# Two graph-attention layers on one core: gathers moved ahead of a norm's root in the first graph, means written in place, and one graph's row of Q made by TensorE

## The chip, the cores and the metric

The kernel runs on one core of a Trainium2 chip. The metric is the device time of one execution in microseconds; lower is better. A time below is the median of several runs, and beside it stands one further execution that was profiled.

## The reference, cut to what matters

The input is x of 16 graphs of 1024 nodes with 256 features, and one adjacency matrix of 1024 x 1024. There are two layers, each with a layer norm in front and a residual behind. The core of it:

```python
h = jnp.maximum(_layernorm(x), 0.0)
# layer 0
out = relu(h @ mlp1_w + mlp1_b);  residual = out            # 256 -> 512
out = elu(_gat(relu(out), None, W_fc, a_fc)) + residual     # dense attention: every node with every node
out = relu(out @ mlp2_w + mlp2_b); residual = out           # 512 -> 256
out = elu(_gat(relu(out), adj, W_hand, a_hand)) + residual  # masked attention
x = x + relu(out)
# layer 1
h = jnp.maximum(_layernorm(x), 0.0)
x = x + relu(masked attention of h with adj, W, a)
```

A `_gat` computes `h = inp @ W`, two numbers per node `f1 = h @ a[:F]` and `f2 = h @ a[F:]`, the scores `leaky_relu(f1[i] + f2[j])`, a softmax over j, and `elu(att @ h)`. All arithmetic is float32.

## The kernel before, in words

Nodes lie on partitions: a graph is 8 tiles of 128 nodes (`NT`), or two halves of 4 tiles (`TH`). Every graph goes through norm, mlp1, dense attention (class `Dense`), mlp2, masked attention a (`Gnn0`), a second norm and masked attention b (`Gnn1`). Neighbouring graphs overlap.

**Dense attention without the 1024 x 1024 matrix.** Because leaky_relu has two slopes, a node's sum over all others is one part over the nodes with a large f2 and one over those with a small f2. The kernel sorts the rows of h by f2: `rank` counts on DVE, `scatter` writes the rows to DRAM in order (an indirect DMA from POOL), `read_sorted` reads them back as `xs`. `sum_before` and `sum_behind` make running sums on DVE, `write_table` and `carry` write them to two tables in DRAM, `fine` and `coarse`. How many nodes lie on one side of node i comes from `sign` (a Sign activation with an accumulator on ACT, one for each tile of nodes) and `count`. Then `gather` (line 642) fetches for each tile of nodes a row of `fine` for each node, and adds a row of `coarse` to it, both by indirect DMAs that POOL issues. `share` (lines 654 to 657, DVE) makes the factors, `mean` (line 664 on ACT, line 666 on DVE) the weighted mean `hp` of 513 columns, `merge` (lines 713 to 717: TensorE transposes, a minimum on DVE, two exponentials on ACT) and `merge_end` (line 723 on DVE, line 724 on POOL) apply elu and add it to `resT`. `mlp2` (line 731) needs all four chunks c of a half of `resT`.

Graph 0 is special. Its first half (4 tiles) is computed in the direct way, `product` (line 695) and `product_mean` (lines 702 to 706), because TensorE has nothing else to do while the tables are made; its second half goes by the tables. `split` is true for graph 0 alone. Its sums lie in `got`, two buffers of two tiles each, which have the tag "hm" (two buffers in all); the means lie in tiles with the tag "hp" (four buffers), which both halves use.

**Rows of Q.** Masked attention needs exp of a per-node value as a row on all partitions. For graphs 1 to 14 (`AHEAD`), `send` transposes it to a line, copies it on ACT and stores it to DRAM (lines 243 to 246), and `row(True)` reads it back on SP's queue to all 128 partitions (line 360). For graphs 0 and 15, `row` makes it by eight TensorE transposes of a broadcast column (line 238) and two copies on ACT (line 365). `weight` (line 375, DVE) makes the attention weights from the row, `product` (line 385) multiplies them.

**What sets the order.** Everything is written out by hand in a table of steps with due times:

```python
def at(lo, hi, steps):
    for i, step in enumerate(steps):
        table.append((lo + (hi - lo) * i / len(steps), len(table), step))
```

The steps run in the order of these times when the program is made, and TensorE, DVE, ACT and SP take their instructions in exactly that order. POOL's instructions, the issue of indirect DMAs among them, keep the table's order too, except that scatters may pass each other. A due time is only a place in that order: an instruction starts when its operands are there and what is ahead of it on its engine is done.

The lines of graph 0's ramp that the change touches, before:

```python
def first_norm(t0, b):                       # called as first_norm(0, 2) for the third graph
    n = norm1[b]
    lo = t0 - (62 if b == 2 else 33.5)
    at(lo, lo + 1, n.stats_steps(0))         # four bn_stats/bn_aggr on DVE, then the root on POOL
...
gathers(d, 1, START + 108, START + 114)      # START is -168; d is graph 0
at(START + 135, START + 135, [partial(d.share, 1)])
at(START + 135.5, START + 137, each(d.mean, [1], range(TH)))
merges(START + 138.2, d, 1)
at(START + 144, START + 158, each(e.sign, range(NT)))    # e is graph 1
```

Here `stats_steps(0)` stands at START + 106, so the root (lines 267 and 268) comes ahead of graph 0's gathers on POOL.

Of the kernel before, what the change touches and what calls it, by code (L numbers as in the profile page):

```python
# [8 lines left out]
F32 = mybir.dt.float32  # L9
# [8 lines left out]
P = 128  # L18
# [13 lines left out]
def fast_path(ctx: ExitStack, tc: tile.TileContext, alarm, x, adj, w1, b1, w2, b2, w_fc, a_fc,  # L32
# [24 lines left out]
    NT = N // P  # L57
# [3 lines left out]
    TH = HALF // P  # L61
    R = H + 2
    K = H + 1
# [3 lines left out]
    work = ctx.enter_context(tc.tile_pool(name="work", bufs=2))  # L67
# [154 lines left out]
# [3 lines that stand above are left out]
# [212 lines left out]
    class Dense:  # L437
# [221 lines left out]
        def mean(self, h, u):  # L659
            n = TH // len(self.got[h])  # L660
            got, den = self.got[h][u // n][:, u % n, :], self.dens[h]
            name = f"{self.b}_{h}_{u}"
            part = work.tile([P, K], F32, tag="part", name=f"part_{name}")
            nc.scalar.activation(part, got[:, :K], AF.Copy, scale=den[:, 1, u:u + 1])
            hp = self.hps[h, u] = work.tile([P, K], F32, tag="hp", name=f"hp_{name}", bufs=TH)
            nc.vector.scalar_tensor_tensor(hp, got[:, K:], den[:, 0, u:u + 1], part,
                                           op0=OP.mult, op1=OP.add)

# [104 lines left out]
    def each(f, *ranges):  # L773
        out = [()]
        for r in ranges:
            out = [o + (i,) for o in out for i in r]
        return [partial(f, *o) for o in out]

    def first_norm(t0, b):

        n = norm1[b]
        lo = t0 - (62 if b == 2 else 33.5)
        at(lo, lo + 1, n.stats_steps(0))
        at(t0 - 13, t0 - 9, n.stats_steps(1))
        n.turn_at(t0 - (14.5 if b == 2 else 22), 0, 4 if b == 2 else 7)
        n.turn_at(t0 + 0.2, 1, 4)
# [49 lines left out]
    def gathers(d, h, lo, hi):  # L836
        at(lo, lo + 4, each(d.gather, [h], [0], range(TH)))
        at(hi, hi + 7, each(d.gather, [h], [1], range(TH)))
# [20 lines left out]
    def merges(lo, d, h):  # L859
        at(lo, lo + 9.2, each(d.merge, [h], range(HC)))  # L860
        at(lo + 2.5, lo + 11.7, each(d.merge_end, [h], range(HC)))

    def second_mlp(t0, b, after=0):
        d, m = dense[b], gnn0[b]
        for i, lo in enumerate((102.5, 104.8, 113, 116.5)):
            lo += t0 - 3.4 * last(b)
            at(lo, lo, [partial(d.mlp2, i // FC, i % FC)])
        t0 += after
        at(t0 + 135, t0 + 142, each(m.project, range(NT)))
        at(t0 + 141.9, t0 + 141.9, [m.extremes])  # L870

    def weights(m, t, n, lo, hi):
        at(lo, hi, each(m.weight, [t], [n], range(NT)))

    def masked_first(t0, b):
        m, n = gnn0[b], norm2[b]
        at(t0 + 1, t0 + 1, [m.vectors])
        lo = t0 + 11
        if b in AHEAD:
            at(t0 + 3.4, t0 + 3.4, [m.send])  # L880
            at(t0 + 6, t0 + 6, [partial(m.row, True)])
            lo += 7
        else:
            at(t0 + 4, t0 + 4, [m.row])
        at(t0 + 4.5, lo - 1, each(m.scale, range(NT)))
        weights(m, 0, 2, lo - 5.5, lo - 1)
        at(t0 + 10, t0 + 10, [partial(load_again, b)])
        if last(b, 2):
            for q, start in enumerate((0.5, 2, 4.2, 5.5)):
                at(t0 + start, t0 + start, [partial(dense[b].natural, q)])  # L890
        else:
            at(t0 + 4.5, t0 + 11, each(dense[b].natural, range(NT // 2)))
        pairs = [(t, 2) for t in range(0, NT, 2)]
        if last(b):
            pairs[-1:] = [(NT - 2, 1), (NT - 1, 1)]
        for t, n_t in pairs:
            start = lo + 3.5 * t
            at(start, start + 3.5 * n_t, each(m.product, [t], [n_t], range(NT)))
            if t:
                weights(m, t, n_t, start - 5.5, start + 1)  # L900
        for t in range(NT):
            end = lo + 7.2 + 7 * (t // 2) + 0.6 * (t % 2)
            if last(b) and t == NT - 2:
                end -= 3.5
            at(end, end, [partial(m.finish, t)])
            at(end + 1.2, end + 1.2, [lambda t=t: m.combine(t, dense[b].o_nat)])
            if last(b) and t >= NT - 2:
                at(end + 2.6, end + 2.6, [lambda t=t: m.add(t, dense[b].o_nat, nc.vector)])
                end -= 2
            at(end + 5.2, end + 5.2, [lambda t=t: m.update(t, xs[b])])  # L910
            end += 5.6 if last(b) else 6.2 if b == 0 else 9
            at(end, end, [partial(n.stats, t)])
        at(lo + 25 - 3.4 * last(b), lo + 25 - 3.4 * last(b), [partial(n.root, 0)])
        lo += 33.1 if last(b) else 35.5 if b == 0 else 38.5
        at(lo, lo, [partial(n.root, 1)])

    def last(b, n=1):
        return b >= NB - n
# [58 lines left out]
    AHEAD = range(1, NB - 1)  # L977
# [4 lines left out]
    START = -168.0  # L982
    n, d = norm1[0], dense[0]
# [34 lines left out]
    for t in range(TH):  # L1018
        lo = START + 95 + 7.1 * t
        at(lo, lo + 7, each(d.product, [t], range(NT)))  # L1020
        at(lo + 8.2, lo + 8.2, [partial(d.product_mean, t)])
    at(START + 100, START + 107, each(d.weight, [1], range(NT)))
    gathers(d, 1, START + 108, START + 114)
    e = dense[1]
    at(START + 95.5, START + 95.5, [e.columns])
    at(START + 98.5, START + 98.5, [e.row, e.highest])
    at(START + 99, START + 118, each(e.rank, range(NT)))
    at(START + 118, START + 118, [less_columns])
    merges(START + 125, d, 0)
    at(START + 135, START + 135, [partial(d.share, 1)])  # L1030
    at(START + 135.5, START + 137, each(d.mean, [1], range(TH)))
    merges(START + 138.2, d, 1)
    second_mlp(START + 39, 0, -13)
    at(START + 123.4, START + 141, each(e.project, range(NT), [0]))
    scatters(e, START + 126, START + 142)
# [1 line left out]
    at(START + 142.5, START + 142.5, [e.read_sorted])  # L1037
    at(START + 76, START + 76, [partial(load_first, 2)])
    first_norm(0, 2)
    at(START + 147, START + 147, [e.sums_begin])  # L1040
    at(START + 144, START + 158, each(e.sign, range(NT)))
    for h in range(2):
        at(START + 150 + 3 * h, START + 150 + 3 * h, [partial(e.sums_weights, h)])
        at(START + 151 + 5 * h, START + 156 + 5 * h, each(e.sum_before, tiles(h)))
# [6 lines left out]
    for b in range(NB):  # L1051
        base, after_base = base_of(b), base_of(b + 1)
        masked_first(base, b)
        second_norm(base, b)
        pairs = range(0, NT, 2)
# [25 lines left out]
        if b + 3 < NB:  # L1081
            lo = after_base - PERIOD + 86
            at(lo, lo, [partial(load_first, b + 3)])
            first_norm(after_base, b + 3)
# [433 lines left out]
def two_layer_gat(tc, *args):  # L1518
    nc = tc.nc
    with tc.tile_pool(name="alarm", bufs=1) as pool:  # L1520
        alarm = pool.tile([1, 1], I32, name="alarm")
        fast_path(tc, alarm, *args)
        with tc.If(nc.values_load(alarm[0:1, 0:1], min_val=0, max_val=1,
                                  skip_runtime_bounds_check_because="it is 0 or 1") > 0):
            general_path(tc, *args)
# [24 lines left out]
```

## Time and profile before

| | |
|---|---|
| median of 3 runs | 2344.05 us (2342.45 to 2348.07) |
| the profiled execution | 2359.75 us, its span 2357.9 us |
| TensorE matmul busy | 2268.6 us, 96% of the span |
| VectorE (DVE) busy | 1625.7 us, 69% |
| ScalarE (ACT) busy | 1241.3 us, 53% |
| GpSimd (POOL) busy | 951.4 us, 40% |
| bytes read from and written to HBM | 227.40 and 126.30 MB |
| the ramp, 100 to 185 us | graph 0's dense attention, graph 1's sort |
| graph 14's masked attention a | begins at about 2124 us |

The span runs from the first to the last instruction of the profiled execution. Its parts add up to more than the span, because the engines work side by side. A timeline lists instructions in order of time: start, length, engine, line, operation, output and inputs, shape, count, and in brackets the engine's idle time just before and what ended it. PEclk is the share of its full clock that TensorE was granted. PE is TensorE, and a matmul in float32 has more than one record.

### The profile page before, as it was taken

Reading aid. Unit: us, or ns where it says so; the run is one execution under the profiler, and the core shown is the slowest. Engines: PE = TensorE matmul, PEld = TensorE weight load, DVE = VectorE, ACT = ScalarE, POOL = GpSimd, SP = SyncE. Lnnn points to the kernel's source line nnn. Section 1 sums busy time; section 2 is a strip of 40 time slices with the busy share of each in tenths; the row PEclk is TensorE's granted clock in tenths of the full one; section 3 lists DMA queues with packets and bytes.
Section 4 is the critical chain, followed back from the end, with each engine's and each line's share of the span. In section 5 each row is a group of like instructions: output and inputs, shape, how many; then the busy total and the mean of one; then the engine's idle time right before and its main releaser. Section 6 shows DMA issues by size and latency. Waiting matters only on the chain. (4 is left out here: it accounts for less than half of the span.)

```text
span 2357.9 us, 30868 instructions
## 1 busy us (share of the span) xinstructions
PE 2268.6 (96%) x9955; PEld 1747.4 (74%) x9955; DVE 1625.7 (69%) x4535; ACT 1241.3 (53%) x2744; POOL 951.4 (40%) x1212
## 2 busy tenths in 40 slices
PE   8989999999999999999999999999999999999888
PEld 6667787777878778786776877777786876877666
DVE  6666685866858567685866867576685856767655
ACT  5345655647365463745546374554736546373442
POOL 1153435354443536334263543526444353533420
PEclk9999999999999999999999999999999999999999
DMA  4658366572656747366573745657265673737500
GB/s 173 165 159 210 72 176 165 167 193 97 200 118 175 180 143 184 97 187 161 172 187 113 186 115 165 174 161 181 91 195 143 174 184 125 185 95 182 140 21 27
DMA packets 150874, 355.81 MB, mean 151 GB/s; under 512 B 11224, under 2 KB 62760, under 8 KB 146608
## 3 DMA queue, kind: packets, MB, share of 16 engines
q1 hardware_dynamic: 104080, 189.58, 28.8%
q0 software_dynamic: 45952, 163.99, 26.3%
q8 instruction: 82, 1.34, 0.2%
q14 instruction: 88, 0.72, 0.1%
q10 hardware_dynamic: 672, 0.17, 0.0%
HBM read 227.40 MB, written 126.30 MB: 150 GB/s over the span
## 5 line engine op out<-in xcount | busy, mean ns | idle before, releaser
L385 PE MATMUL ob<-hmb,attb 128*128 128x257 f32 x2048 | 467.9, 386 | 21.4 <-DVE attb L375 17.0
L470 PE MATMUL h<-wfc_sb,resT 128*128 128x257 f32 x2048 | 465.7, 380 | 0.0
L385 PE MATMUL oa<-hma,atta 128*128 128x258 f32 x2048 | 454.7, 381 | 7.2 <-DVE atta L375 7.1
L385 PEld LDWEIGHTS ob<-hmb,attb 128*128 128x128 f32 x2048 | 387.2, 192 | 88.1 <-DVE attb L375 21.0
L385 PEld LDWEIGHTS oa<-hma,atta 128*128 128x128 f32 x2048 | 387.6, 190 | 67.0 <-issue 5.1
L470 PEld LDWEIGHTS h<-wfc_sb,resT 128*128 128x128 f32 x2048 | 379.5, 190 | 53.5 <-issue 0.7
L724 POOL TENSOR_TENSOR resT<-resT,e 128x512 f32<-128x512 f32 x128 | 163.6, 1278 | 371.4 <-DVE e L723 330.1
L375 DVE SCALAR_TENSOR_TENSOR atta<-rowsa,qwda,edge 128x256 f32<-128x256 f32 (+1 forms) x520 | 268.4, 545 | 27.6 <-PE oa L385 12.8
L413 POOL TENSOR_TENSOR posa<-posa,onat 128x256 f32<-128x256 f32 x118 | 98.7, 836 | 461.8 <-ACT posa L401 461.6
L375 DVE SCALAR_TENSOR_TENSOR attb<-rowsb,qwdb,edge 128x256 f32<-128x256 f32 (+1 forms) x536 | 247.9, 503 | 8.9 <-PE ob L385 5.5
L427 ACT ACTIVATE rb<-ob,recb 128x256 f32<-128x256 f32 x128 | 59.0, 475 | 346.1 <-DVE recb L425 329.4
L456 PE MATMUL m<-hT,w_sb 128*128 128x512 f32 x512 | 235.0, 598 | 0.5 <-ACT posa L401 0.5
L731 PE MATMUL m<-resT,w_sb 128*128 128x512 f32 x512 | 230.3, 596 | 4.3 <-POOL resT L724 4.3
L642 POOL DMA_INDIRECT got<-coarse,k x124 | 200.7, 1618 | 38.9 <-issue 37.7
L400 ACT ACTIVATE ea<-oa,reca 128x256 f32<-128x256 f32 x128 | 60.7, 474 | 271.2 <-DVE reca L397 262.1
L715 DVE TENSOR_SCALAR e<-hpT 128x512 f32<-128x512 f32 x128 | 88.3, 690 | 134.3 <-PE hpT L713 101.4
L731 PEld LDWEIGHTS m<-resT,w_sb 128*128 128x128 f32 x512 | 93.9, 191 | 106.3 <-issue 90.9
L456 PEld LDWEIGHTS m<-hT,w_sb 128*128 128x128 f32 x512 | 92.6, 193 | 95.9 <-issue 91.7
L642 POOL DMA_INDIRECT got<-fine,k x124 | 125.7, 1013 | 74.4 <-DMA fine<-xs 41.9
L530 POOL DMA_INDIRECT sorted<-hnat,place x128 | 131.9, 1030 | 39.6 <-issue 20.5
L553 ACT ACTIVATE junk<-r,fs 128x1024 int8<-128x1024 f32 x124 | 142.4, 1149 | 8.7 <-POOL fs L474 5.3
L716 ACT ACTIVATE e<-e 128x512 f32<-128x512 f32 x128 | 80.7, 631 | 84.2 <-DVE e L715 84.1
(186 smaller groups left out, 3445.8 us busy)
## 6 DMA issues: line engine op xcount, KB each, us to landing
xs<-sorted SPq DMA_DIRECT2D x32, 1028.0 KB
fine<-tt SPq DMA_DIRECT2D x32, 1026.0 KB
fine<-xs SPq DMA_DIRECT2D x32, 1026.0 KB
x<-in_x_dram SPq DMA_DIRECT2D x16, 1024.0 KB
xn<-in_x_dram SPq DMA_DIRECT2D x15, 1024.0 KB
out_dram<-x SPq DMA_DIRECT2D x28, 512.0 KB
coarse<-carry SPq DMA_DIRECT2D x32, 256.5 KB
r<-row_r SPq DMA_DIRECT2D x14, 512.0 KB
```

Source lines behind the costliest of these rows:

```text
L375: nc.vector.scalar_tensor_tensor(a_t[:, :n * P], self.rows[:, i], self.qwd[:, 1, j:j + 1], edge[:, j, i], op0=OP.max, op1=OP.mult)
L385: nc.tensor.matmul(self.out[t][:, :F + self.ONES], lhsT=self.att[t0, j][:, (t - t0) * P:(t - t0 + 1) * P], rhs=self.hm[:, j, 2:2 + F + sel ...
L413: adder.tensor_add(pos, pos, o_nat[:, t, :])
L456: nc.tensor.matmul(ps, lhsT=w1_sb[:, kc, c * P:(c + 1) * P], rhs=hT[:, kc, h * HALF:(h + 1) * HALF], start=(kc == 0), stop=(kc == FC - 1))
L470: nc.tensor.matmul(ps[:, :F + 1], lhsT=self.resT[:, kc, t * P:(t + 1) * P], rhs=wfc_sb[:, kc, g, :], start=(kc == 0), stop=(kc == HC - 1))
L530: made = nc.gpsimd.indirect_dma_start(out=sorted_d[self.b % 2], out_offset=bass.IndirectOffsetOnAxis(ap=self.place[:, t:t + 1], axis=0), i ...
L553: nc.scalar.activation(junk, self.r2, AF.Sign, bias=self.fs[:, 0, t:t + 1], accum_out=self.signs[:, t:t + 1])
L642: nc.gpsimd.indirect_dma_start(out=got[u // n][:, u % n, :], out_offset=None, in_=(coarse_d if coarse else fine_d)[self.b % 2][:, :], in_o ...
L715: nc.vector.tensor_scalar_min(e, ps, 0.0)
L716: nc.scalar.activation(e, e, AF.Exp)
L724: nc.gpsimd.tensor_add(dst, dst, e)
L731: nc.tensor.matmul(ps, lhsT=w2_sb[:, kc, c * P:(c + 1) * P], rhs=self.resT[:, kc, h * HALF:(h + 1) * HALF], start=(kc == 0), stop=(kc == H ...
```

## The change

Five edits, four of them in graph 0's ramp. (1) The means of graph 0's second half are written over the gathered sums instead of into a tile of their own. (2) The third graph's first four statistics and their root move from START + 106 to START + 119, and graph 0's gathers from START + 108 and 114 to START + 101 and 106, so that on POOL the gathers now stand ahead of the root. (3) The share, the means and the merges of that half get earlier places, the means of the first half a slightly earlier one. (4) The eight Sign activations of graph 1 move from START + 144 to 158 to START + 130 to 150. (5) For graph 14 the row of Q is made by TensorE, as for graphs 0 and 15, while its other due times stay those of a graph in `AHEAD`.

```diff
@@ mean
-            hp = self.hps[h, u] = work.tile([P, K], F32, tag="hp", name=f"hp_{name}", bufs=TH)
+            hp = self.hps[h, u] = got[:, K:] if self.split else work.tile(
+                [P, K], F32, tag="hp", name=f"hp_{name}", bufs=TH)
             nc.vector.scalar_tensor_tensor(hp, got[:, K:], den[:, 0, u:u + 1], part,
                                            op0=OP.mult, op1=OP.add)
@@ first_norm
-        lo = t0 - (62 if b == 2 else 33.5)
+        lo = t0 - (49 if b == 2 else 33.5)
@@ masked_first
         if b in AHEAD:
+            lo += 7
+        if b in AHEAD and not last(b, 2):
             at(t0 + 3.4, t0 + 3.4, [m.send])
             at(t0 + 6, t0 + 6, [partial(m.row, True)])
-            lo += 7
         else:
             at(t0 + 4, t0 + 4, [m.row])
@@ the ramp
-        at(lo + 8.2, lo + 8.2, [partial(d.product_mean, t)])
+        at(lo + 7.6, lo + 7.6, [partial(d.product_mean, t)])
     at(START + 100, START + 107, each(d.weight, [1], range(NT)))
-    gathers(d, 1, START + 108, START + 114)
+    gathers(d, 1, START + 101, START + 106)
...
-    at(START + 135, START + 135, [partial(d.share, 1)])
-    at(START + 135.5, START + 137, each(d.mean, [1], range(TH)))
-    merges(START + 138.2, d, 1)
+    at(START + 130, START + 130, [partial(d.share, 1)])
+    at(START + 130.5, START + 135, each(d.mean, [1], range(TH)))
+    merges(START + 136, d, 1)
...
-    at(START + 144, START + 158, each(e.sign, range(NT)))
+    at(START + 130, START + 150, each(e.sign, range(NT)))
```

What this does to the order of each engine, in the ramp: on POOL the eight gathers pass the root, and two of the adds of line 724 pass a scatter's copies and a memset. On DVE the four statistics move behind the ranks, the share and the first two means move ahead of the last merge of the first half. On ACT the eight Signs stand singly between the exponentials, the copies of line 472 and the parts of line 664, instead of together behind them: two Signs stand ahead of the last of the four parts. On TensorE the transposes of the second half's first chunk move ahead of tile 6 of graph 1's projection (line 470). SP's order is the same. In graph 14, eight transposes take the place of one, two copies on ACT the place of a copy and a store, and one transfer leaves SP's queue.

## The prediction

> **What bounds the kernel now.** The page first: TensorE is busy 96% of the span, so only its gaps can be won, and the edits touch two stretches: graph 0's ramp (about 100 to 185 us) and graph 14's masked attention (about 2124 us on).
>
> ```profile
> PE 2268.6 (96%) x9955; PEld 1747.4 (74%) x9955; DVE 1625.7 (69%) x4535; ACT 1241.3 (53%) x2744; POOL 951.4 (40%) x1212
> ```
>
> Then TensorE's timeline in the ramp; a bracket is idle time and what ended it.
>
> ```profile
> 124.80 2.01 PE L695 MATMUL od<-hnat,attd 128*128 128x257 f32 x8 [1.55 <-ACT hpd L705]
> ...
> 143.07 5.37 PE L470 MATMUL h<-wfc_sb,resT 128*128 128x257 f32 x24
> 150.01 0.30 PE L713 MATMUL hpT<-ident,hp 128*128 128x128 f32 x1 [1.57 <-DVE hp L666]
> 150.59 0.33 PE L713 MATMUL hpT<-ident,hp 128*128 128x128 f32 x1 [0.27 <-DVE hp L666]
> 152.65 0.33 PE L713 MATMUL hpT<-ident,hp 128*128 128x128 f32 x1 [1.73 <-DVE hp L666]
> 153.31 0.47 PE L713 MATMUL hpT<-ident,hp 128*128 128x128 f32 x1 [0.34 <-DVE hp L666]
> 153.58 3.28 PE L470 MATMUL h<-wfc_sb,resT 128*128 128x257 f32 x8
> ...
> 167.91 1.13 PE L731 MATMUL m<-resT,w_sb 128*128 128x512 f32 x2 [1.14 <-POOL resT L724]
> 169.95 2.03 PE L731 MATMUL m<-resT,w_sb 128*128 128x512 f32 x2 [0.92 <-POOL resT L724]
> ...
> 176.90 7.14 PE L322 MATMUL pa<-wh_sb,oT 128*128 128x258 f32 x32
> ```
>
> The gaps are 1.55, 0.52 (at 136.4), 3.91 and 2.06 us. Two groups run at half rate (153.58: 3.28 for what takes 1.90 elsewhere), as the view by windows shows (PE busy first, PEclk third from the end):
>
> ```profile
> 149.55:152.96 3.41, 0.94 (x3) 0.41 (x3) 3.28 (x4) 1.60 (x3) 3.05 (x4) 1.00 0.20 77
> 152.96:156.37 3.41, 3.07 (x9) 2.50 (x9) 0.99 (x2) 1.35 (x2) 2.27 (x4) 0.50 0.20 77
> 170.03:173.44 3.41, 3.41 (x10) 2.27 (x11) 2.40 (x6) 3.38 (x10) 0.00 (x0) 0.50 0.00 0
> ```
>
> POOL's timeline says why graph 0's second half is late, DVE's what its means cost:
>
> ```profile
> 122.24 0.23 POOL L267 TENSOR_SCALAR rstd<-mv 128x4 f32<-128x4 f32 x1 [48.03 <-DVE mv L263]
> ...
> 135.45 1.53 POOL L642 DMA_INDIRECT got<-coarse,k  x1 [0.30 <-issue]
> ```
> ```profile
> 146.95 1.85 DVE L655 TENSOR_TENSOR den<-den,got 128x2 f32<-128x2 f32 x1
> ...
> 149.12 4.14 DVE L666 SCALAR_TENSOR_TENSOR hp<-got,den,part 128x513 f32<-128x513 f32 x4
> ```
>
> The root holds the gathers until 123.79; the last one, issued at 135.45, lands at 144.5.
>
> Graph 14 (timelines of TensorE, DVE and POOL):
>
> ```profile
> 2136.94 14.59 PE L385 MATMUL oa<-hma,atta 128*128 128x258 f32 x64 [2.44 <-DVE atta L375]
> ...
> 2182.75 2.71 PE L385 MATMUL ob<-hmb,attb 128*128 128x257 f32 x8 [3.43 <-DVE attb L375]
> ```
> ```profile
> 2136.31 0.48 DVE L375 SCALAR_TENSOR_TENSOR atta<-rowsa,qwda,edge 128x256 f32<-128x256 f32 x1 [3.02 <-DMA rowsa<-row_a]
> ```
> ```profile
> 2173.22 0.99 POOL L642 DMA_INDIRECT got<-fine,k  x1 [3.67 <-DMA fine<-xs]
> ```
>
> [...] 0.94 us busy of 3.41, then 3.41 us at 0.50. [...] The 1.85 us above (0.17 to 0.20 elsewhere) lies across POOL's L724 of 147.49 to 148.78[...] In graph 14 the SP queue's transfers land in the order of their issue (rowsa 2136.2, x 2140.1, the tables 2148.0, 2157.8, 2165.1, 2172.5)[...]
>
> **Part 1, the ramp.** No instruction is added or taken away; the order changes on TensorE, DVE, ACT and POOL, while SP's stays as it is.
>
> DVE loses four L262/L263 pairs (2.17 us) from among the ranks, so the recip of od_1 (124.02) comes at 121.85 and od_3 no longer waits: TensorE gains 1.55. The pairs go behind b_less, 129.3 to 131.5, where DVE was idle; recd_3 (131.9) just clears them. POOL's root (1.4 us) follows the gathers at about 132.5, and the copies of fs and the scatters queued behind it wait for hnat at 134.4 anyway, so the gathers' new wait costs nothing there; were the tables 13 us later, it would.
>
> The gathers stand first on POOL but need the tables: the fine landing ends at 119.1, the coarse at 121.2 (landing semaphores). With the old spacings, the last lands near 140.0, 4.5 us earlier. Their 1.0 share of the DMA engines falls in 119 to 140, where the SP queue moves nothing.
>
> The means no longer take hp buffers, which merge 3's transposes held until 143.2, and go ahead of that merge's minimum. In exchange got is held until hpT_1_3, near 161; the next writers of these buffers are hma's copies from 172 on, so that costs nothing. After h_3's copy (ACT, 143.12 less 1.55 = 141.57) ACT now runs in this order: copy 0.27, Sign 1.26, two parts 1.26 (to 144.45); the exps of e_0_3, which wait for hp 0, hp 1 (0.70 each) and L715 on DVE, to 147.2; copy 0.25, Sign 1.26, two parts, to 150.06. The last hp ends at 150.85. TensorE is through h_5 at 145.0, so it waits **5.9 us** in hpT_1_0, more than before, and ends it at 151.05. Before, the same transposes ended at 153.6, but h_6 (1.73) was already done: the merge itself brings 0.8 us net.
>
> From there to pa TensorE has h_6 and h_7 (3.46), three hpT (1.30), four m (13.75), nt (0.87) and 0.4 of small losses: 19.8 (the same sum for before leaves 0.4 unexplained), and one half-rate window, which I put at 1.4 (the one at 153.58 cost 3.28 - 1.90 = 1.4; ends: 0, and 2.1 if the drop spans two). It reaches pa at 151.05 + 21.2 = 172.3. The 2.06 us of waits on resT go: eight Signs (8 x 1.26 = 10.1 us of ACT) leave 165 to 179 and L724 of e_1_3 ends at 166.2, a microsecond ahead of m_10's last quarter (POOL: two L724 pass ahead of fs 7 and of the memset of tt, both of which have time); with them goes the second half-rate window (1.7). Gain at pa: 176.9 - 172.3 = **4.6 us**, ends 2.5 and 6.5.
>
> Does it stay? Scatter 7 leaves POOL at 158.6 (before 158.29), so graph 1's sorted rows land no earlier, but bd on ACT comes at 167.7 instead of 171.3, because the Signs are done; the sums start 3.4 us earlier. Its table writes on SP's queue move with them. The first half of graph 1's gathers lands at 230.9 and is used at 238.9, so the missing 1.2 us is covered.
>
> **Part 2, graph 14.** Removed: a transpose, a 0.24 us copy, the 4 KB store, SP's wait until 2131.73 and a 512 KB broadcast. Added: eight transposes (0.87 from graph 15's rows, 1.09 with the tail) and 1.08 us of ACT copies (graph 15's L365). TensorE loses only 0.25, since it waited 0.28 for ACT there. The load of x, which stood behind that wait on SP, is issued earlier, but follows xs in the ring. rowsa is ready at 2128 instead of 2136.2; DVE reaches atta after the sums it has in front at 2133.3, before TensorE ends ob (2134.75). So 2.44 - 0.25 = 2.2 us.
>
> Next to be late is the DMA ring: rowsa took from 2133.5 to 2136.2 on its slower engines, which then stay in arrears until fine<-xs lands at 2172.5. Without it that landing is 2.7 us earlier, and it paces POOL's gathers, the adds queued behind them, x, attb and the 3.43 us gap. Gain here **2.7**, ends 1.5 and 3.5.
>
> **Sum.** 4.6 + 2.7 = 7.3 us of the profiled execution's 2359.75 (span 2357.9 and 1.85 around it), to 2352.45. The median of the runs, 2344.05, lies 15.7 lower; the same difference gives **2336.8 us**, 0.31% faster. A measurement of this kernel tells about 0.3%, here 7.0 us, from no change.
>
> **The rivals.**
> *Wait moved back* (0.20): L724 reaches m_10 late after all, with its half-rate window, or, as if the gathers did nothing of what is said, they land at 144.5 as now and hp 0 starts at 145.25 instead of 143.9. Each costs 1.4 to 3.7; about 2340.4. For it: only 1 us of slack. Against: ACT sheds 10.1 us there.
> *No half rate* (0.20): a window's phase splits TensorE's wait, or ACT is quicker, and the drop is saved too, with up to 1.3 more: gain near 10, 2334.
> *Half rate stays* (0.08, slower): with ACT feeding it in pieces from 148 to 172, TensorE fails window after window to look busy. Each costs 1.71; from the fifth further window the kernel is slower than now, and nine give 2336.8 + 15.4 = 2352.2. Against: before, each drop lasted one window.
>
> **How the numbers follow.** Main case 0.45, own range 2335 to 2339, half of it beyond 7.0 us; 0.07 lies outside these cases. Faster 0.23 + 0.20 + 0.04; same 0.22 + 0.20 + 0.01; slower 0.08 + 0.02. The range 2331 to 2345 leaves out the slow case and the far ends.
>
> **What would show it.** Right: od_3 without a gap; gathers from 119.3; one TensorE wait of some 6 us ahead of h_6, ended by DVE on L666; no wait on resT at m; pa near 172.3; oa in graph 14 without a gap, and POOL's fine<-xs wait near 3. Wrong: hpT_1_0 ready by 146 (ACT mis-sized), or after 154; two half-rate windows or more; the 3.43 us gap unchanged.

## The result, and the profile after

| | before | after |
|---|---|---|
| median of 13 runs each | 2349.09 us (2340.48 to 2350.78) | 2338.85 us (2332.90 to 2343.30) |
| the profiled execution | 2359.75 us, span 2357.9 | 2332.90 us, span 2331.2 |

The ratio of the times is 0.9961, with a 95% interval of 0.9952 to 0.9969: 9.2 us faster (7.3 to 11.3; the medians alone differ by 10.2). The prediction was a gain of 7.3 us. Nine of the 13 times of before lie between 2347.6 and 2350.8 us, the other four between 2340.5 and 2344.1. The two profiled executions differ by 26.7 us, far more than the medians: the one of before is slower than all 13 of its runs, the one of after is the fastest of its 13. From pa of graph 1 to pa of graph 14, where nothing was changed, they took 1823.8 and 1809.3 us. So the spans are not compared below, only stages.

Some names: od_3 is the last of the four tiles of graph 0's direct half, h_6 is tile 6 of graph 1's projection, hpT_1_0 are the transposes of chunk 0 of graph 0's second half, m is mlp2, and pa and oa are the projection and the weighted sum of masked attention a (ob of b).

The engines' busy times from the page: the same work within noise, TensorE 97% busy instead of 96.

```profile
PE 2260.4 (97%) x9962; PEld 1742.7 (75%) x9962; DVE 1625.0 (70%) x4535; ACT 1240.5 (53%) x2745; POOL 950.8 (41%) x1212
```

TensorE's timeline of the kernel after, in the ramp:

```profile
117.68 7.99 PE L696 MATMUL od<-hnat,attd 128*128 128x257 f32 x36
...
147.30 0.41 PE L714 MATMUL hpT<-ident,got 128*128 128x128 f32 x2 [1.74 <-issue]
150.87 0.44 PE L714 MATMUL hpT<-ident,got 128*128 128x128 f32 x1 [3.17 <-DVE got L667]
151.54 0.47 PE L714 MATMUL hpT<-ident,got 128*128 128x128 f32 x1 [0.23 <-DVE got L667]
151.81 3.17 PE L470 MATMUL h<-wfc_sb,resT 128*128 128x257 f32 x8
...
161.29 7.03 PE L732 MATMUL m<-resT,w_sb 128*128 128x512 f32 x16
```

od runs without its gap of 1.55 us. There is one place of waiting, ahead of h_6, of 1.74 + 3.17 + 0.23 = 5.14 us (before 3.91 in the same place), and m has no wait on resT. The 5.9 us of the prediction are the stretch from the end of h_5 to the last mean, with three transposes in it: that stretch took 6.0 us, from 145.56 to 151.54. One group runs at half rate (3.17 us for what takes 1.90); before there were two such places.

POOL's timeline: the gathers are issued from 118.70, the last at 129.86 (before 123.79 and 135.45), and the root follows them.

```profile
118.70 0.99 POOL L642 DMA_INDIRECT got<-fine,k  x1 [43.84 <-DVE attd L688]
...
129.86 1.53 POOL L642 DMA_INDIRECT got<-coarse,k  x1 [0.30 <-issue]
132.27 0.23 POOL L267 TENSOR_SCALAR rstd<-mv 128x4 f32<-128x4 f32 x1 [0.88 <-DVE mv L263]
```

Graph 14, TensorE's timeline and then POOL's: the gap of 2.44 us at oa is gone, and so, against the prediction, is the one of 3.43 us at ob: of it 0.11 is left. POOL does not wait for fine.

```profile
2115.74 14.08 PE L385 MATMUL oa<-hma,atta 128*128 128x258 f32 x64
...
2160.47 5.83 PE L385 MATMUL ob<-hmb,attb 128*128 128x257 f32 x24
```
```profile
2147.85 0.99 POOL L642 DMA_INDIRECT got<-fine,k  x1 [0.16 <-issue]
```

**How the stages are compared.** Executions reach the ramp up to 2 us apart, so the ramp is measured from TensorE's last wait on carry (L626, 106.46 us before, 107.14 after) to the first pa of graph 0. "Gaps" are TensorE's recorded idle times in a stretch, "half" the time in it at PEclk 0.50. Graph 14's stretch runs from its pa to that of graph 15. The change in us is the ratio times the median of before in the runs taken beside that kernel, with its interval: 2339.99 to 2342.4 us for the experiments (all on one chip, the candidate on another), 2349.09 for the result. The changed kernel itself was not run beside the experiments, so its 9.2 us can be compared with their numbers only loosely.

| kernel | change, us | ramp | gaps | half | graph 14 | gaps | half |
|---|---|---|---|---|---|---|---|
| before | | 70.44 | 8.05 | 6.83 | 138.0 | 17.9 | 10.2 |
| after | -9.2 (-11.3 to -7.3) | 65.33 | 5.64 | 3.41 | 131.4 | 13.6 | 3.4 |
| ramp only | -4.7 (-6.3 to -3.3) | 65.41 | 5.75 | 3.41 | 135.7 | 14.5 | 13.7 |
| row 14 only | -1.6 (-3.3 to 0) | 70.42 | 8.06 | 6.83 | 134.3 | 13.5 | 10.2 |
| Signs back | -1.9 (-4.2 to +0.5) | 64.51 | 4.61 | 3.41 | 135.3 | 13.1 | 13.7 |
| Signs behind | -7.3 (-10.3 to -4.4) | 64.51 | 4.61 | 3.41 | 131.5 | 13.6 | 3.4 |
| gathers back | -5.6 (-7.7 to -3.7) | 67.93 | 7.05 | 6.83 | 133.0 | 13.6 | 6.8 |
| hp tiles | -6.8 (-9.1 to -4.7) | 66.37 | 5.61 | 6.83 | 135.2 | 13.1 | 13.7 |
| spare load | -10.3 (-14.0 to -6.3) | 66.72 | 5.60 | 6.83 | 132.7 | 13.5 | 6.8 |
| all rows | -7.7 (-10.3 to -4.9) | 65.22 | 5.61 | 3.41 | 132.1 | 13.0 | 6.8 |
| share early | -8.4 (-11.7 to -5.2) | 62.12 | 3.26 | 0 | 132.9 | 13.5 | 6.8 |
| means back | -5.2 (-7.0 to -3.3) | 69.75 | 6.85 | 10.24 | 135.3 | 13.1 | 13.7 |
| statistics alone | -1.6 (-3.3 to 0) | 68.32 | 6.51 | 6.83 | 138.1 | 16.0 | 13.7 |
| candidate | -10.5 (-13.3 to -7.5) | 62.13 | 3.26 | 0 | 135.5 | 13.1 | 13.7 |

Of the ramp's 70.44 - 65.33 = 5.1 us, the gaps gave 8.05 - 5.64 = 2.4. The other 2.7 lie outside the gaps. m and nt, where the half-rate window from 170.03 is gone, took 15.02 and 1.65 us before and 13.57 and 0.87 after, 2.2 us less; od took 0.3 us less; h with its transposes, where a half-rate window stays, took 0.2 us less. The gain is kept: from pa of graph 0 to pa of graph 1 both executions took 115.9 us.

### The profile page after: what moved, and what is told of

It is laid out like the page before. It is cut to its first block, busy times and chain, and to the rows that moved or that the text cites. A ratio compares the mean times of both kernels' runs of the same rounds, so it can differ in the third digit from the quotient of the medians.

```text
span 2331.2 us, 30884 instructions
## 1 busy us (share of the span) xinstructions
PE 2260.4 (97%) x9962; PEld 1742.7 (75%) x9962; DVE 1625.0 (70%) x4535; ACT 1240.5 (53%) x2745; POOL 950.8 (41%) x1212
## 5 line engine op out<-in xcount | busy, mean ns | idle before, releaser
L385 PE MATMUL ob<-hmb,attb 128*128 128x257 f32 x2048 | 462.8, 383 | 10.8 <-DVE attb L375 6.7
L725 POOL TENSOR_TENSOR resT<-resT,e 128x512 f32<-128x512 f32 x128 | 163.7, 1279 | 367.0 <-DVE e L724 325.7
```

The lines of the kernel that those rows point to most:

```text
L385: nc.tensor.matmul(self.out[t][:, :F + self.ONES], lhsT=self.att[t0, j][:, (t - t0) * P:(t - t0 + 1) * P], rhs=self.hm[:, j, 2:2 + F + sel ...
L725: nc.gpsimd.tensor_add(dst, dst, e)
```

## The experiments

**The parts apart.** The first kernel is the changed one with the old lines for graph 14, the second the one before with the new lines (cut to what counts):

```diff
-        if b in AHEAD and not last(b, 2):      # in the first kernel; the reverse in the second
+        if b in AHEAD:
             at(t0 + 3.4, t0 + 3.4, [m.send])
             at(t0 + 6, t0 + 6, [partial(m.row, True)])
```

> The changed kernel with graph 14's row of Q still sent through DRAM, as before; the ramp is all of the change. Theory of the prediction (the two parts are independent, 4.6 us from the ramp): 4.6 us faster than before (2.5 to 6.5), pa of graph 0 at 172 to 173 us of the span, and graph 14 with its two gaps of 2.4 and 3.4 us as before. Rival (the ramp's gain is given back later, and graph 14 carries all of the measured 9 us): within 1 us of before.

Measured: 4.7 us faster (3.3 to 6.3); the ramp is that of the changed kernel, so this part stands as predicted. Graph 14 brought a surprise. TensorE's timeline and POOL's, with the row sent as before:

```profile
2120.28 15.85 PE L385 MATMUL oa<-hma,atta 128*128 128x258 f32 x64 [2.32 <-DVE atta L375]
...
2166.35 5.37 PE L385 MATMUL ob<-hmb,attb 128*128 128x257 f32 x24
```
```profile
2153.03 0.99 POOL L642 DMA_INDIRECT got<-fine,k  x1 [0.16 <-issue]
```

The gap at oa is there, the gap at ob is not, and POOL does not wait for fine, although the 512 KB broadcast is in the ring. In the trace's DMA records the last table write ends 49.3 us after pa here, and POOL comes to the gather at 53.1. In the profiled execution of before it ended at 55.7: its writes of 2052 bytes took 165 ns each on average, here 131. In that execution POOL waited for fine in graphs 2, 4, 6, 10 and 12 too, 0.9 to 3.8 us each, with gaps of 0.8 to 3.6 us at ob; in the other 13 traces it did so in no graph from 1 to 14. So the gap of 3.43 us goes with the slow table writes of that execution.

> The kernel before with graph 14's row of Q made by TensorE; nothing of the ramp. Theory of the prediction (2.2 us for the wait at oa, then the ring ends 2.7 us earlier): 2.7 us faster than before (1.5 to 3.5), with 2.9 us left of the gap of 3.43 us. Rival, from the profile of the changed kernel (the ring ends some 9 us earlier in graph 14, counted from pa, and that gap is gone): 4.5 to 6.5 us faster than before, with less than 1 us left of that gap, so that the two parts add up to about 9 us.

Measured: 1.6 us faster (0 to 3.3). That holds the 2.7 of the prediction and excludes the 4.5 to 6.5 that the two profiles suggest. The gap at ob is gone as well, as it is where the row is sent; so it speaks for neither theory. The two parts add up to 6.3 us; their intervals together reach some 2.2 us to either side, and meet that of the whole (7.3 to 11.3), which was measured apart from them.

**The Signs, put back and put behind the parts.**

```diff
-    at(START + 130, START + 150, each(e.sign, range(NT)))
+    at(START + 144, START + 158, each(e.sign, range(NT)))      # Signs back
+    at(START + 135.2, START + 152, each(e.sign, range(NT)))    # Signs behind
```

> The changed kernel with the eight Signs of graph 1 back at START + 144 to 158. Theory (the Signs' leaving the time of m is what took away the waits on resT and the second half-rate window): hpT_1_0 comes 2.5 us earlier, for two Signs of 1.26 us no longer stand ahead of the parts, but 1.1 and 0.9 us of waits on resT and 1.7 us of half rate return: about 1.3 us slower than the changed kernel. Rival (ACT's pace ahead of the means is all that counts): 2.5 us faster than the changed kernel, with pa of graph 0 near 170 us.

Measured: graph 1's pa, counted from the wait on carry, comes at 182.77 instead of 181.20, 1.6 us later. The size is as expected, the way is not: the waits on resT at m stay away. TensorE waits at pa for oT, ACT's relu of m, which stands behind Signs:

```profile
175.99 1.14 PE L322 MATMUL pa<-wh_sb,oT 128*128 128x258 f32 x4 [1.66 <-ACT oT L735]
```

And hpT_1_0 comes only 1.0 us earlier (gaps of 4.10 instead of 5.14), not 2.5. In device time the kernel is 1.9 us faster than before (-0.5 to 4.2), which is 5.4 us less than with the Signs behind the parts, below; the traces of the two differ by only 1.7 us up to graph 1's pa, and where the rest comes from is open.

> The changed kernel with the eight Signs of graph 1 at START + 135.2 to 152, so behind the four parts on ACT but still ahead of m. Theory (two Signs ahead of the parts are 2.5 us of TensorE's 5.1 us of waiting for hpT_1_0, and the Signs are still gone when m runs): 2.5 us faster than the changed kernel, pa of graph 0 near 170 us. Rival (the Signs between the exps of the second merge make resT late and a wait at m takes the place of the one won): no more than 0.7 us either way.

Measured: the same 1.0 us less waiting ahead of h_6, pa 0.8 us earlier, but graph 1's pa only 0.1 us earlier (181.08). No gain to be seen in device time: 7.3 us faster than before (4.4 to 10.3). So what times the means is not mainly the Signs. With the Signs away ACT stands still ahead of the parts, for share on DVE:

```profile
143.75 1.34 ACT L664 ACTIVATE part<-got,den 128x513 f32<-128x513 f32 x2 [1.48 <-DVE den L657]
```

In the changed kernel this wait is 0.35 us, behind the Sign. DVE's timeline of the changed kernel shows why share ends late:

```profile
140.57 0.68 DVE L724 SCALAR_TENSOR_TENSOR e<-hpT,e 128x512 f32<-128x512 f32 x1
141.16 0.15 DVE L654 TENSOR_TENSOR den<-got,qd 128x2 f32<-128x2 f32 x1
...
141.75 2.04 DVE L657 TENSOR_TENSOR den<-den,qd 128x2 f32<-128x2 f32 x1
```

Share starts when L724 of the first half's merge is done, without a wait on the gathers. The last product for the first two tiles takes 2.04 us instead of 0.16, across POOL's L725 of 142.48 to 143.76. It is no single case: in all 14 traces together 27 of the small two-input instructions of share (L654, L655 and L657 here) took over 0.6 us (3 and 2 of 158 in the profiled executions of before and after, where no other took over 0.29), and each of the 27 ended 0.02 to 0.03 us after the end of one of POOL's adds of 1.3 us. In 12 of the 27, this one among them, the record on DVE begins 0.5 to 0.7 us ahead of the add's; why it then lasts to the end of the add was not tried.

**The gathers and the statistics back.**

```diff
-        lo = t0 - (49 if b == 2 else 33.5)
+        lo = t0 - (62 if b == 2 else 33.5)
-    gathers(d, 1, START + 101, START + 106)
+    gathers(d, 1, START + 108, START + 114)
```

> The changed kernel with the second half's gathers (START + 108 and 114) and the statistics of the third graph's norm (t0 - 62) where they were, so that the root stands ahead of the gathers again. Theory (the landing of the gathers then ends last again, at 144.5 us instead of 139.3, and od_3 waits 1.5 us for recd again): share starts 3 us later than in the changed kernel and hpT_1_0 comes about 2 us later: pa of graph 0 near 174.5 us. Rival (ACT's and DVE's order, not the gathers, sets the means: in the changed kernel DVE takes up share at 141.2, two us after the landing): pa within 0.6 us of 172.5.

Measured: the ramp takes 2.6 us longer, as expected, but not by the landing. od_3 waits 1.55 us again, which moves all that follows; the waiting ahead of h_6 is 4.98 us instead of 5.14; and the half-rate stretch behind it lasts two windows instead of one, about 1.2 us. The last gather is issued at 135.93, and DVE's share still stands directly behind L724, with no wait on a DMA:

```profile
142.48 0.68 DVE L724 SCALAR_TENSOR_TENSOR e<-hpT,e 128x512 f32<-128x512 f32 x1
143.07 0.15 DVE L654 TENSOR_TENSOR den<-got,qd 128x2 f32<-128x2 f32 x1
```

So what counts in this edit is that the statistics leave the ranks. By an estimate from these times, with od_3's wait gone the old gathers would come about a microsecond late for share's second part; that was not tried by itself.

**Tiles for the means.**

```diff
-            hp = self.hps[h, u] = got[:, K:] if self.split else work.tile(
+            hp = self.hps[h, u] = work.tile(
                 [P, K], F32, tag="hp", name=f"hp_{name}", bufs=TH)
```

> The changed kernel with the second half's means written to hp tiles, as before, and not over the gathered sums. Theory (the tiles come free when the transposes of the first half's last merge end, near 142 us, and the first mean is written at 144.6): no difference, pa of graph 0 at 172.5 within 0.3 us. Rival (the means in place are what the ramp's gain needs): pa 1 to 2.5 us later.

Measured: the same gaps to 0.05 us. The ramp is 1.0 us longer in this execution, and again its half-rate stretch is two windows, in a kernel that waits at the same places for the same time. Writing in place shows no gain here.

**The load without the wait.** Row 14 by TensorE, and 512 KB that nobody reads on SP's queue:

```diff
+        elif b in AHEAD:
+            at(t0 + 4, t0 + 4, [m.row])
+            at(t0 + 6, t0 + 6, [m.spare])
...
+            for i in (slice(0, HALF), slice(HALF, N)):
+                unread = work.tile([P, K], F32, tag="hp", name=f"spare{i.start}", bufs=TH)
+                nc.sync.dma_start(unread[:, :HALF], row_d[self.which][(self.b + 1) % 2][:, i]
+                                  .to_broadcast([P, HALF]))
```

> The changed kernel, with graph 14's row made by TensorE, and beside it 512 KB of another row that stands ready in DRAM, sent over SP's queue at the place of the old broadcast into two tiles that nothing reads: the load stays, the wait for it goes. Theory of the prediction (the broadcast put the ring 2.7 us in arrears, which it kept to the last landing of fine): the table writes end 2 to 3 us later than without it, POOL waits for fine again, ob has a gap of 2 to 3 us, and the kernel is 2.5 us slower than the changed one. Rival, from the run with the ramp alone, whose row was sent and which had no gap at ob (the gap of 3.43 us came from slow table writes in the one profiled execution of before): no gap at ob over 0.5 us, POOL does not wait for fine, and the time is that of the changed kernel within 1 us.

Measured: no gap at ob (0.10), no wait for fine, 10.3 us faster than before (6.3 to 14.0, from 4 runs), as the rival has it. The last table write does end later, 48.8 us after pa where the other kernels with this row have 43.6 to 46.5, and POOL comes to the gather at 50.5. The arrears in the ring are real; in this execution nobody waits for them.

This kernel's ramp is that of the changed one, instruction for instruction, with gaps of 5.60 us for 5.64, and took 1.4 us longer. The view by windows shows that the clock differs. After, then spare load; PE busy is the second number, PEclk the third from the end:

```profile
147.54:150.95 3.41, 0.25 (x3) 0.08 (x1) 0.89 (x2) 3.41 (x8) 2.30 (x4) 1.00 0.16 60
150.95:154.37 3.41, 3.18 (x8) 2.36 (x9) 1.82 (x3) 2.44 (x4) 1.49 (x3) 0.50 0.22 82
154.37:157.78 3.41, 3.41 (x20) 2.78 (x19) 1.37 (x3) 2.73 (x6) 2.63 (x5) 1.00 0.20 77
```
```profile
146.29:149.70 3.41, 0.41 (x2) 0.20 (x2) 0.54 (x2) 3.38 (x7) 2.33 (x4) 1.00 0.20 77
149.70:153.11 3.41, 2.70 (x7) 2.04 (x8) 2.42 (x4) 2.57 (x6) 1.62 (x4) 0.50 0.23 82
153.11:156.53 3.42, 3.42 (x11) 2.75 (x11) 0.78 (x2) 2.04 (x5) 1.62 (x5) 0.50 0.20 77
```

After, the first half-rate window was 3.18 us busy, and the next was at full rate. With the spare load the wait reached 0.5 us into that window, which was 2.70 us busy, and the next stayed at half rate too.

**Every row by TensorE.**

```diff
-        if b in AHEAD and not last(b, 2):
+        if False:
```

> The changed kernel with the row of Q made by TensorE in graphs 1 to 13 too. Theory (there TensorE waits for nothing that the row holds up, so eight transposes of 0.11 us for one, 0.76 us, are added to each of 13 graphs): 10 us slower than the changed kernel, so about 1 us slower than before. Rival (what the broadcasts leave free on SP's queue shortens other waits by as much): within 3 us of the changed kernel, so 6 us or more faster than before.

Measured: 7.7 us faster than before (4.9 to 10.3), as the rival has it. From pa of graph 1 to pa of graph 14 it took 1803.4 us, spare load 1805.0. The transposes are there (104 more on rowspsa, 91 in all, 0.76 us for each of 13 graphs). The groups of that stretch show what shrank, first spare load, then all rows (busy and mean, then idle before):

```profile
L391 PE MATMUL ob<-hmb,attb 128*128 128x257 f32 x1664 | 373.0, 382 | 2.5 <-DVE attb L381 2.2
...
L282 PE MATMUL nt<-ident,hn 128*128 128x128 f32 x408 | 57.9, 278 | 5.9 <-DVE hn L272 5.9
```
```profile
L385 PE MATMUL ob<-hmb,attb 128*128 128x257 f32 x1664 | 367.6, 380 | 0.3 <-DVE attb L375 0.3
...
L282 PE MATMUL nt<-ident,hn 128*128 128x128 f32 x408 | 57.7, 278 | 3.5 <-DVE hn L272 3.5
```

The gaps at ob and nt fall by 2.2 and 2.4 us, and ob's own time by 5.4: with the spare load 59 of the 1625 steps from one matmul record of ob to the next took over 0.26 us, with all rows 6, and the others 0.22. These are waits too short to be listed as gaps. By the brackets DVE set the pace in those places, and TensorE's added 9.9 us lie in its waiting.

**Share early.** Share ahead of the first L724, two parts ahead of the third merge's exps on ACT, the four means ahead of its L724, Signs behind; its core:

```diff
+    at(START + 127.4, START + 127.4, [partial(d.share, 1)])
+    for u, lo in enumerate((127.42, 127.44, 130.2, 130.22)):      # L664 on ACT
+        at(START + lo, START + lo, [partial(d.mean, 1, u, False)])
+    for u, lo in enumerate((130, 130.02, 130.4, 130.42)):         # L667 on DVE
+        at(START + lo, START + lo, [partial(d.mean_add, 1, u)])
```

> The changed kernel with share ahead of the first L724 on DVE (DVE then waits for the gathers' landing), two parts ahead of the third merge's exps on ACT and two behind them, all four means ahead of that merge's L724, and the Signs behind at START + 135.2 to 152. Theory (in the changed kernel it is DVE's and ACT's order and a 2.0 us L657 beside POOL's L725, not the landing, that end TensorE's 5.1 us of waiting for hpT_1_0): TensorE waits some 1 to 2 us there in all, in pieces too short for a half-rate window; from the last wait on carry (L626, near 107 us) to pa of graph 0 it takes 60 to 61.5 us instead of 65.3, and the kernel is 3.5 to 5 us faster than the changed one, some 13 us faster than before. Rival (ACT has as much work as before and then holds oT or resT at m or pa): 62.5 us or more, or graph 1's pa no more than 1.5 us earlier.

Measured: TensorE's timeline has four small waits, 2.65 us in place of 5.14, and no half-rate window behind them:

```profile
140.72 0.63 PE L726 MATMUL hpT<-ident,hpd 128*128 128x128 f32 x4 [1.07 <-DVE e L736]
...
147.57 0.63 PE L726 MATMUL hpT<-ident,got 128*128 128x128 f32 x4 [0.58 <-PE h L470]
```

The ramp is 62.12 us, 3.2 less than in the changed kernel, which shows that order and not the landing sets the means in the changed kernel. Half of it is given back: at nt behind pa TensorE waits 1.14 us for hn, whose statistics stand behind tt on DVE, and graph 1's pa comes only 1.6 us earlier (179.64). In device time nothing is to be seen of it: 8.4 us faster than before (5.2 to 11.7).

**The means back.**

```diff
-    at(START + 130, START + 130, [partial(d.share, 1)])
-    at(START + 130.5, START + 135, each(d.mean, [1], range(TH)))
-    merges(START + 136, d, 1)
+    at(START + 135, START + 135, [partial(d.share, 1)])
+    at(START + 135.5, START + 137, each(d.mean, [1], range(TH)))
+    merges(START + 138.2, d, 1)
```

> The changed kernel with share, the means and the second merge back at START + 135, 135.5 and 138.2, behind the first half's last merge; means still in place, gathers, statistics and Signs as changed. Theory (of the 5.1 us that the stretch from the last wait on carry to pa became shorter, 70.4 to 65.3, the statistics gave 1.5 and this order the most of the rest): 2 to 3.5 us later at pa than the changed kernel, 67.3 to 69 us for that stretch. Rival (the Signs gave the rest, the order nothing): 65 to 66.7 us.

Measured: a ramp of 69.75 us, 4.4 more than the changed kernel and more than expected, and 5.2 us faster than before in the time (3.3 to 7.0). The waits on resT at m return, although the Signs are where the change put them:

```profile
167.47 1.13 PE L732 MATMUL m<-resT,w_sb 128*128 128x512 f32 x2 [1.14 <-POOL resT L725]
169.51 1.55 PE L732 MATMUL m<-resT,w_sb 128*128 128x512 f32 x2 [0.92 <-POOL resT L725]
```

With them comes the window at half rate at 170, and the first stretch is two windows long. So the earlier share, means and merges took away the waits at m; the Signs had to go because oT would have been late next.

**The statistics alone**, on the kernel before:

```diff
-        lo = t0 - (62 if b == 2 else 33.5)
+        lo = t0 - (49 if b == 2 else 33.5)
```

> The kernel before with one edit: the statistics of the third graph's norm at t0 - 49 instead of t0 - 62, so that four L262/L263 pairs leave the ranks and the root stands behind the gathers. Theory (od_3's wait of 1.5 us goes and nothing gives it back): the stretch from the last wait on carry to pa of graph 0 takes 68.9 us instead of 70.4, and the kernel is 1.5 us faster than before. Rival (TensorE waits for the same means later, and what it gains at od_3 it loses at hpT_1_0): 70 to 70.5 us, no gain. A stretch under 68 us would say that the gathers' earlier start counts by itself.

Measured: od_3's 1.55 us are gone, the other gaps are as before, the ramp is 2.1 us shorter, 1.6 us in the time (0 to 3.3). The 0.6 us over lie outside the gaps, where the half rate stands elsewhere: the waits at m, 1.14 and 0.93, fell into two windows here, each over 2.3 us busy, and no drop followed, while the first half-rate stretch lasts two windows. Before, both waits fell into the window from 166.61 to 170.03, which was 1.35 us busy. The gathers are issued from 116.64 in this kernel, because the root stands behind them, and land at 137.6 instead of 144.5; yet share begins at 145.13, its place in DVE's order, instead of 146.10.

**A candidate**, from what stayed late: with share early, the second half's statistics ahead of tt, and graph 14's scales on ACT earlier.

```diff
-        at(t0 - 13, t0 - 9, n.stats_steps(1))
+        at(*(t0 - 17.28, t0 - 17.2) if b == 2 else (t0 - 13, t0 - 9), n.stats_steps(1))
...
+            first = [] if last(b) else each(m.scale, range(2))
+            at(lo + 7.15, lo + 7.2, first)
-            at(lo + 9.3, lo + (10.5 if last(b) else 17), each(m.scale, range(NT)))
+            at(lo + 9.3, lo + (10.5 if last(b) else 15.2), each(m.scale, range(len(first), NT)))
```

> A candidate: the kernel with share early, and two more moves. The second half's statistics of the third graph's norm go ahead of tt on DVE (they stood behind tt, which waits for xs; TensorE waited 1.1 us for hn at nt near 178 us). Graph 14's scales on ACT: two right behind its second attention's vectors, the other six up to lo + 15.2 instead of lo + 17 (TensorE waited 1.5 us at ob for the last of them, behind exps that DVE held up). Theory: the wait at nt in graph 0 and the second wait on hmb in graph 14 go, 1.1 and 1.5 us; from the last wait on carry to graph 1's pa 178.5 us (179.6 with share early, 181.2 in the changed kernel); the kernel 2.5 us faster than with share early and some 4 us faster than the changed one: 12 to 13 us faster than before. Rival (TensorE waits at ob for attb, whose DVE has the same work to do, and the next nt waits for hn anyway): no faster than with share early, which was 8.4 us (5 to 12) faster than before.

Measured: the waits at nt and on hmb (ACT's scaled rows) are gone. But graph 1's pa comes at 180.14, not at 178.5 and later than with share early, with a half-rate window from 229.56 on the way. And at ob DVE's attb is late in the place of hmb, as the rival has it:

```profile
2182.69 2.90 PE L385 MATMUL ob<-hmb,attb 128*128 128x257 f32 x12 [1.57 <-DVE attb L375]
```

10.5 us faster than before (7.5 to 13.3). That it beats the changed kernel or share early is not shown: the intervals lie over each other.

## Why the prediction was right, and where it was not

**The ramp, 4.6 us: right, 5.1 by the trace, 4.7 (3.3 to 6.3) by the runs of that part.** Its terms:

- od_3's 1.55: as predicted, and by the statistics (it goes in the kernel with the statistics alone, and comes back with them).
- Half rate: as predicted. The window that stays was put at 1.4 us; h_6 took 3.17 instead of 1.90, so 1.3. The one that goes was put at 1.7; m and nt took 2.2 less. The half microsecond over is, by difference, what TensorE lost around the two waits on resT; the prediction carried such small losses of before (0.4) over, and they went with the waits. From the end of hpT_1_0 to pa it took 20.5 us, predicted 21.2: this is the term that was mis-sized. In other executions of the same instructions the first drop lasts two windows and costs 1.0 to 1.4 more, 2.3 to 2.7 in all; the prediction's end for that case was 2.1.
- The wait at hpT_1_0: 6.0 for 5.9, counted as the prediction counts. Set back by the 0.68 us by which this execution reaches the ramp later, ACT's first two parts end at 144.5 and DVE's last mean at 150.8 (predicted 144.45 and 150.85). In this there is luck: the sum goes along ACT alone and leaves out DVE's share with its 2.04 us beside POOL. Share held the parts up by 0.35 us, and the Sign ahead of them happened to end 0.3 us earlier than predicted. That the two run so close is why taking both Signs away won only 1.0 us.
- "The 2.06 us of waits on resT go: eight Signs leave 165 to 179": they go, by another cause. With the Signs back they stay away; with the means back they return. The Signs' leaving prevents a wait of 1.7 us on oT at pa, and is worth 1.6 us by the trace.
- "The last lands near 140.0": 139.3. But the landing was not what ended last, neither before nor after: it came 1.6 and 1.9 us ahead of share, which stood in DVE's order behind other work. The gathers' early start and the means in place have no measured share in the gain.
- "Does it stay?": yes. Graph 1's pa comes 5.1 us earlier, as graph 0's does (181.20 instead of 186.29 from the wait on carry).

**Graph 14, 2.7 us: inside its interval (0 to 3.3), with half of its reasons not borne out.** The 2.2 us at oa stand: oa starts 18.1 to 18.3 us after pa in the traces with TensorE's row, and 20.3 to 20.6 in the three with the row sent. "Next to be late is the DMA ring" was read off one execution whose table writes were slow. In the two others with the same row, and in the one with the spare load, the ring is in arrears and the last write ends 1.7 to 4.1 us ahead of POOL. So there was no gap of 3.43 us to be won in those, and its 0.11 after the change is not shown to be a gain of the change. What the row is worth in an execution with slow writes was not tried.

**The sum.** 7.3 predicted, 9.2 measured (7.3 to 11.3), at the edge. The two parts by themselves gave 6.3, and the kernels whose gaps differ from those of the changed one by 1 us or less (Signs behind, hp tiles, spare load) 6.8 to 10.3. So a part of the 9.2 may not be the change's: before took 2349.1 us where the result was measured and 2340.0 to 2342.4 beside the experiments, and its profiled execution lost time to slow table writes in graphs that the change does not touch. Whether its other runs there did too is open. The median was forecast from 3 runs of before as 2336.8; that 2338.85 comes so close is in part luck, since the median of before rose by 5.0 us with 13 runs, and the two medians lie 2.9 us further apart than forecast, which takes part of it back. The rivals: no wait moved back on to the gathers, and half rate did not stay window after window. "No half rate" (near 10 us) is close in number, but the first window did stay; it went only where share stands early.

## What to carry to other kernels

When an engine stands still for a transfer in a trace, find out whether the instruction that reads the data is waiting or only queued behind something else on its own engine; here the gathers landed 1.9 us before anyone asked. A gap in one profiled execution may belong to that execution alone: look for it in a second one and in stages that the change does not touch, compare stages from a common event, and set gaps and clock apart. Added work on the busiest engine can be free where it already waits for a slower one, as the rows of Q were in graphs 1 to 13 (9.9 us of transposes more, yet 1803.4 us from pa of graph 1 to that of graph 14, against 1805.0 with the spare load).

## What the runs showed of the hardware that was not expected

TensorE's half rate went with where a wait lay in time, not with its length alone. In the profiled executions of before and after every change of the granted clock after the first drop lies a whole number of times 3.41 us behind it (in after 1, 24, 25, 626 and 627), and up to the kernel's end the drops of all 14 traces last 3.41 or 6.83 us. Counted in windows of 3.41 us in step with the drops, every full-rate window with more than 2.0 us of gaps was followed by a half-rate one in these traces (42 of them), none with less than 1.2 us was, and between these both happened (26 dropped). In graph 14 the time outside the gaps, with TensorE's row, was 117.8, 119.3, 120.8 and 122.2 us with one, two, three and four such windows: 1.5 us each. The kernels with one and with four have the same instructions there, so this alone moves a run by up to 4.4 us, about as much as the ramp's part of the change.

The table writes' speed differs between neighbouring graphs, too: in the profiled executions of before and after, writes of 2052 bytes took 117 to 138 ns on average in the stretches that begin with pa of an odd graph, and 133 to 165 ns in those of the even graphs from 2 on. In the other kernels that send the row the difference is smaller (averages over graphs 1 to 13 of 113 to 116 ns in the odd stretches and 122 to 130 in the even ones). With every row made by TensorE it is gone: 100 to 106 ns in all graphs from 1 to 13. So it goes with the broadcast rows in the ring; how they do it was not tried.
